# A four-layer graph network on one core: the written-out order of its operations set anew

## The chip, the cores and the metric

One core of one Trainium2 chip runs the whole program in one launch. The metric is device time in microseconds. Before the change the median of three runs is 2291.22 us (2289.76 to 2291.41).

The engines are named as in the profile: PE is TensorE's matmul, PEld its weight load, DVE is VectorE, ACT is ScalarE, POOL is GpSimd, and SP is SyncE, which here only issues DMAs.

## The reference

128 graphs of 64 nodes with 256 features (`x`), and an adjacency matrix per graph (`adj`), go through four layers. Each layer is followed by a residual and a layer norm. In float32, and cut to what matters:

```python
# layer 0: gated graph network, 5 steps
A = (adj != 0); h = x
for l in range(5):
    m = einsum('bnd,de->bne', h, weight[l])
    agg = einsum('bij,bid->bjd', A, m)
    h = gru_cell(agg, h, w_ih, w_hh, b_ih, b_hh)
x = layernorm(x + h * mask[..., None])
# layer 1: aggregate, two-layer network with an RMS norm between
agg = epsilon * x + adj @ x
h = silu(rmsnorm(agg @ W1 + b1, rms_weight))
x = layernorm(x + h @ W2 + b2)
# layer 2: tangent map, aggregate, map back onto the ball
x = layernorm(x + project(expmap0(adj @ logmap0(x))))
# layer 3: attention
h = x @ W_w.T + W_b
e, f = h @ a_w[:256], h @ a_w[256:]
u = adj * exp(e[:, :, None] + f[:, None, :] + a_b[0])
x = layernorm(x + (u / u.sum(2, keepdims=True)) @ h)
```

## The kernel before, in words

**Tiles and groups.** Two graphs share a block of 128 rows, so there are 64 blocks, and four blocks make a group: 16 groups. `group(g)` builds a group's operations. Layer 0 and most of layer 1 are built for all four blocks at once; the rest of the group is built twice, for a half of the blocks each. So the program is 49 streams: one for set-up and three per group. Buffers exist for three groups (`NF = 3`), and PSUM has eight banks of 512 columns that are handed out in turn.

**What a group does.** In layer 0, each of five steps (`gated`) aggregates (`ps_agg`, L396), multiplies by gate weights (`p_ga`, `p_gb`, `p_gc` at L915; `p_hx`, `p_hy`, `p_ix`, `p_iy` at L921), and evaluates sigmoids and tanh as tanh on ACT (L968, L1032). Products of 2 by 2 blocks are formed in seven products instead of eight, with sums on DVE (`tA`, `tB`, helper line L434) and additions of PSUM results on DVE (L965, L981, L937). The new state is made on DVE (L434, L1038, L1040), transposed in pieces on DVE (L877, `t`) and moved to rows by four DMAs (`hr`). Layer 1 uses `p_ah`, `p_bh`, `p_ch` (L1098), squares on ACT (L1084) that are summed on POOL (`sqt`, L437), Silu on ACT (L1149), and `p_ox`, `p_oy` (L1173). Layer 2 uses `ps_sup` and many small steps on POOL (`few`, L427; `few_s`, L431). Layer 3 uses `ps_a` and `ps_att`, with the small product at L1386. Layer norms take their sums from accumulators (L800, L817, L822), powers and small steps on POOL, and the scaling `x_n` on ACT or DVE (L419, L420). Additions of a bias row over a whole group run on POOL (`xb` and `x_n` at L437). The last two groups do the small steps on DVE instead, and the last group forms its second product of layer 1 without the seven-product scheme (`ps_o`).

**What sets the order.** No operation is emitted where the code names it. `flow.op` and `flow.either` only record it, in its stream, with an engine, a price in microseconds, what it reads and what it writes. `either` records an operation with two ways, ACT or DVE (`copied`, `scaled`, the `tan` scaling at L1293). When all is recorded, `flow.issue()` emits the operations in the order that the string `ORDER` (L58 to L243) spells, and binds each to the one before it on its engine by an ordering edge that needs no semaphore. Each engine then works through its own operations strictly in that order, and waits by semaphores for its inputs; SP issues its DMAs in that order too. The string is read so:

```python
for c in marks:
    i = at(next(marks)) * n + at(next(marks)) if c == "~" else at(c)
    i, e = divmod(i, len(self.ENGINES))
    i, s = divmod(i, self.AHEAD)
    o, eng = waiting[first + s][self.ENGINES[e]][i], self.ENGINES[e]
```

One mark thus names an engine `e`, a stream `s` counted from the first unfinished one, and the place `i` among the operations of that stream that may run on that engine and have not been taken. A mark of two letters after `~` has a larger number. An `either` operation goes to the engine that the mark names. The order in which PSUM banks are handed out follows the string as well. `placed()` uses neither the prices nor the `port` flags; they are what a planner outside the kernel was given to write the string with.

**The prices.** Before, `act` is priced at 0.22 + 0.00077 n whatever it reads, `scaled` at 0.3 + 0.0008 n on ACT, `dve` at 0.145 + 0.00105 n, `few` and `few_s` at 0.25, PE operations of 256 columns (two instructions each) at 0.433. A `port` flag marks a DVE or POOL operation[...].

## Time and profile before

| what | value |
|---|---|
| median of three runs | 2291.22 us |
| the profiled execution's own time | 2286.62 us |
| its span in the profile | 2284.8 us |
| mean granted PE clock | 0.996 of full speed |
| instructions | 34210 |
| operations in `ORDER` | 13729 |
| DMA traffic | 84.59 MB in 430044 packets |
| `hr` DMAs, issue to landing | 256 of 128 KB, median 3.8 us |
| ACT table loads | 47, 1.28 us each |

Times in the profile are microseconds unless marked ns. A row of a stretch gives its start and end, its length, then for PE, PEld, DVE, ACT and POOL the busy time with the number of instructions, the granted PE clock, the busy share of the DMA engines and the GB/s that they moved. A row in order of time gives start, length, engine, line, operation, output and inputs, and in brackets the idle time of the engine ahead of it with what ended it. A row of a group gives busy time and the mean ns of one, then the idle time ahead of the group. A line such as L437 or L419 belongs to a helper, so the tile names tell which operation is meant.

### The profile page before, as it was taken

The numbers are of one execution on the slowest core, as the hardware profiler recorded it, in microseconds if no ns is written. First come the engines' busy times: TensorE is split into PE (matmuls) and PEld (weight loads), VectorE is DVE, ScalarE is ACT, GpSimd is POOL, SyncE is SP. The second block draws the span as 40 slices with busy tenths as digits, with TensorE's granted clock in tenths as the row PEclk, the third lists the DMA queues.
The fourth block names the chain that finished last, engine by engine and source line by source line (L and its number), as shares of the span: only waits on it lengthen the run. The fifth ranks groups of instructions, "written<-read, shape, count | busy, mean of one in ns | idle before, by whom it ended". The sixth has DMA issues, their size and how long they took to land.

```text
span 2284.8 us, 34210 instructions
## 1 busy us (share of the span) xinstructions
PE 2237.4 (98%) x12050; PEld 1982.7 (87%) x12050; DVE 1827.1 (80%) x3832; ACT 1307.4 (57%) x2856; POOL 536.7 (23%) x827
## 2 busy tenths in 40 slices
PE   9999999999999999999999999999999999999986
PEld 7888898988898898988989889898988989888865
DVE  6787788787787888888888787878888788877886
ACT  3444656665556656556565666656566565654565
POOL 4100213422113213122231212222122231210222
PEclk9999999999999999999999999999999999999998
DMA  6021122112203122121212212212121212211110
GB/s 156 15 37 29 20 31 58 19 27 42 56 13 51 33 31 56 21 38 31 33 42 33 55 19 41 39 29 47 29 40 29 38 41 33 44 29 19 33 19 28
DMA packets 430044, 84.59 MB, mean 37 GB/s; under 512 B 399237, under 2 KB 428961, under 8 KB 429873
## 3 DMA queue, kind: packets, MB, share of 16 engines
q1 hardware_dynamic: 428144, 80.52, 19.9%
q8 instruction: 96, 1.57, 0.3%
q10 hardware_dynamic: 1328, 1.31, 0.2%
q0 software_dynamic: 400, 0.57, 0.1%
q14 instruction: 76, 0.61, 0.1%
HBM read 32.55 MB, written 8.39 MB: 18 GB/s over the span
## 4 chain that ended last, share of the span: by engine, by line
PE 89%; DVE 6%; DMA 1%; ACT 1%; SPq 1%; issue 1%; POOL 0%; ACTq 0%; DVEq 0%; POOLq 0%
PE p_ga L915 23%; PE p_gc L915 11%; PE ps_agg L396 7%; PE p_ix L921 6%; PE p_gb L915 6%; PE p_hx L921 6%; PE p_iy L921 5%; PE p_ox L1173 4%; PE p_hy L921 4%; PE p_ah L1098 4%; PE p_oy L1173 3%; PE ps_a L396 2%; PE p_ch L1098 2%; PE ps_sup L396 1%; PE ps_att L396 1%; PE p_bh L1098 1%
## 5 line engine op out<-in xcount | busy, mean ns | idle before, releaser
L431 POOL TENSOR_SCALAR mv<-st 128x4 f32<-128x4 f32 x56 | 17.5, 313 | 767.6 <-ACT x_n L817 425.2
L915 PE MATMUL p_ga<-hT,w_h 128*128 128x256 f32 x640 | 177.4, 380 | 0.9 <-DVE U L965 0.9
L915 PE MATMUL p_gc<-tA,w_h 128*128 128x256 f32 x640 | 177.4, 380 | 0.0
L915 PE MATMUL p_gc<-tB,w_a 128*128 128x256 f32 x640 | 176.1, 380 | 0.4 <-DVE tB L434 0.4
L915 PE MATMUL p_ga<-tA,w_h 128*128 128x256 f32 x640 | 175.7, 379 | 0.0
L915 PE MATMUL p_ga<-tB,w_a 128*128 128x256 f32 x640 | 171.1, 380 | 0.6 <-DVE tB L434 0.6
L915 PE MATMUL p_ga<-agg,w_a 128*128 128x256 f32 x640 | 170.4, 379 | 0.0
L396 PEld LDWEIGHTS ps_agg<-edge,hr 128*128 128x128 f32 x1024 | 146.2, 191 | 19.2 <-issue 4.9
L419 ACT ACTIVATE hnb<-p_hx,half_b 128x256 f32<-128x256 f32 x202 | 95.1, 472 | 105.7 <-PE p_hx L921 82.5
L968 ACT ACTIVATE U<-U,half_b 128x512 f32<-128x512 f32 (+1 forms) x160 | 94.4, 628 | 106.1 <-DVE U L965 105.9
L396 PE MATMUL ps_agg<-edge,hr 128*128 128x128 f32 x1024 | 150.6, 276 | 4.3 <-DMA hr<-t 2.8
L915 PEld LDWEIGHTS p_ga<-tB,w_a 128*128 128x128 f32 x640 | 120.1, 190 | 16.9 <-DVE tB L434 1.3
L915 PEld LDWEIGHTS p_gc<-tB,w_a 128*128 128x128 f32 x640 | 119.7, 190 | 16.9 <-DVE tB L434 1.2
L915 PEld LDWEIGHTS p_ga<-agg,w_a 128*128 128x128 f32 x640 | 119.1, 190 | 16.1 <-issue 0.7
L915 PEld LDWEIGHTS p_gc<-tA,w_h 128*128 128x128 f32 x640 | 119.0, 190 | 15.5 <-ACT agg L414 0.2
L915 PEld LDWEIGHTS p_ga<-hT,w_h 128*128 128x128 f32 x640 | 116.9, 190 | 15.2 <-DVE U L965 1.3
L915 PEld LDWEIGHTS p_ga<-tA,w_h 128*128 128x128 f32 x640 | 117.5, 190 | 14.2
L968 ACT ACTIVATE V<-V,half_b 128x256 f32<-128x256 f32 (+1 forms) x160 | 88.7, 587 | 68.0 <-DVE V L965 67.8
L834 POOL TENSOR_TENSOR rstd<-ve,pow 128x4 f32<-128x4 f32 (+2 forms) x67 | 80.2, 1197 | 136.2 <-DVE ve L832 124.8
L414 ACT COPY agg<-ps_agg 128x512 f32<-128x512 f32 x133 | 77.2, 582 | 51.1 <-PE ps_agg L396 50.0
L822 ACT ACTIVATE x_n<-y,mv 128x256 f32<-128x256 f32 x168 | 83.4, 499 | 38.4 <-POOL mv L431 38.4
L981 DVE TENSOR_TENSOR V<-p_ix,V 128x256 f32<-128x256 f32 x192 | 80.6, 420 | 27.9 <-PE p_ix L921 24.0
(289 smaller groups left out, 6161.1 us busy)
## 6 DMA issues: line engine op xcount, KB each, us to landing
hr<-t SPq DMA_DIRECT2D x256, 128.0 KB, 3.8
x<-in_x_dram SPq DMA_DIRECT2D x64, 128.0 KB, 2.6
xr<-in_x_dram SPq DMA_DIRECT2D x16, 512.0 KB, 3.5
xs<-in_x_dram SPq DMA_DIRECT2D x120, 64.0 KB, 2.4
out_dram<-x_n SPq DMA_DIRECT2D x15, 512.0 KB, 3.0
x3T<-t SPq DMA_DIRECT2D x56, 128.0 KB, 3.9
edge<-in_adj_dram SPq DMA_DIRECT2D x64, 32.0 KB, 2.5
wm<-in_L_gnn_weight_dram SPq DMA_DIRECT2D x5, 256.0 KB, 4.0
```

Source lines behind the costliest of these rows:

```text
L396: return nc.tensor.matmul(o, lhsT, rhs, start=(k == 0), stop=(k == nk - 1))
L414: flow.either([("ACT", 0.22 + 0.00077 * n, lambda: nc.scalar.copy(o(), i())), ("DVE", 0.145 + 0.00105 * n, lambda: nc.vector.tensor_copy(o ...
L419: flow.either([("ACT", 0.3 + 0.0008 * n, lambda: nc.scalar.activation(o(), i(), AF.Identity, bias=bias(), scale=scale())), ("DVE", 0.145 + ...
L431: pool(0.25, lambda: nc.gpsimd.tensor_scalar(w[0](), x(), s0, s1, op0, *((op1,) if op1 else ())), [w[1]], r)
L822: act(400, lambda b=b: nc.scalar.activation(o[:, b, :], y[:, at + b, :], AF.Square, bias=mv[:, b, 0:1], accum_out=st[:, b, 1:2]), [(o, b), ...
L834: pool(1.25, lambda: nc.gpsimd.tensor_tensor(rstd[:, :m, :], ve[:, :m, :], pow2[:, :m, :NB], OP.pow), [rstd], [ve])
L915: pe(HR, lambda i=i, w=w, c=c: nc.tensor.matmul(ps[:, c * HR:(c + 1) * HR], w[:, m, c * P:(c + 1) * P], v[i][0](), start=first and i == 1 ...
L921: pe(HR, lambda: nc.tensor.matmul(ps[:, j * HR:(j + 1) * HR], w[:, m, :], v[0](), start=first, stop=True, skip_group_check=True), [ps], [( ...
L968: act(HR if len(w) == 1 else R, lambda: nc.scalar.activation(o(), src(), AF.Tanh, bias=half_b[:, i * KD + c:i * KD + c + 1], scale=0.5), w ...
L981: dve(HR + 44, lambda: nc.vector.tensor_add(uu[:, c, half(n)], region(ps, j), uu[:, c, half(n)]), [(uu, (n, c))], [ps, (uu, (n, c))])
L1098: pe(HR, lambda c=c: nc.tensor.matmul(ps[:, c * HR:(c + 1) * HR], w1f[:, w, (2 * q + c) * P:(2 * q + c + 1) * P], v[0](), start=first and ...
L1173: pe(128, lambda j=j, k=k: nc.tensor.matmul(ps[:, i * HR + j * P:i * HR + (j + 1) * P], val(v[k // 2])[:, k % 2, j * P:(j + 1) * P], w2f[: ...
```

## The change

The string `ORDER` is replaced by another (18561 characters before, 18857 after). The set of operations and what each reads and writes stay as they are. Beside it, the prices are changed to durations measured in a trace, for ACT apart by whether an operand lies in PSUM (a bank) or in SBUF, and three operations get the `port` flag: the `edge` comparison (L862), the `tan` scaling on DVE and the small product at L1386. Prices and flags emit nothing.

The diff, with the first line alone of each string:

```diff
-    ORDER = ("EACAAEAg~BrADA#ECA~OX~BOAADAA$AADA$iAAC~N.~Bs~Bt~Bti~OXi~CU~CU~CU~CUi~Bt~Nr~B,~Bt8E8E~B,8l8~FU~Fy~Fy"
...
+    ORDER = ("CEEg~PhD~BNhED~BOiDC~Bs$CAAAAAAAAAAAAAAAAii~Nr~Nr~BO~N.~CU8~B+88~Bt~Bt8$~Bt~BL~Bt88li~BL~FU~FU~FU~FU"
...
+    def in_bank(r):
+        return any((a[0] if isinstance(a, tuple) else a).bank for a in r)
+
+    def on_act(n, r):
+        if n < 32:
+            return 0.26 if in_bank(r) else 0.205
+        return 0.355 + 0.00045 * n if in_bank(r) else 0.28 + 0.00085 * n
+
     def act(n, run, w, r, sets=None):
-        flow.op("ACT", 0.22 + 0.00077 * n, run, w, r, sets=sets)
+        flow.op("ACT", on_act(n, r), run, w, r, sets=sets)
...
     def scaled(n, o, i, scale, bias, w, r, port=()):
-        flow.either([("ACT", 0.3 + 0.0008 * n, ...),
-                     ("DVE", 0.145 + 0.00105 * n, ...)], w, r, port=port)
+        flow.either([("ACT", on_act(n, r) if in_bank(r) else on_act(n + 108, r), ...),
+                     ("DVE", (0.21 if in_bank(r) else 0.145) + 0.00105 * n, ...)], w, r, port=port)
...
     def few(w, x0, x1, op, r):
-        pool(0.25, ...)
+        pool(0.2, ...)
     def few_s(w, x, s0, op0, r, s1=None, op1=None):
-        pool(0.25, ...)
+        pool(0.23, ...)
...
     def pool_sum(n, o, x0, x1, op, w, r):
-        pool(0.24 + 0.00211 * n, ...)
+        pool(0.24 + 0.00203 * n, ...)
...
-            dve(R, lambda: nc.vector.tensor_scalar(ed[:, :NB, :], ...), [ed], [ed])
+            dve(270, lambda: nc.vector.tensor_scalar(ed[:, :NB, :], ...), [ed], [ed], True)
...
-                        dve(HR + 44, lambda: nc.vector.tensor_add(hnb[:, c, half(n)], ...
+                        dve(HR + 6, lambda: nc.vector.tensor_add(hnb[:, c, half(n)], ...
...
-                ("ACT", 0.43, ... tan ...),
-                ("DVE", 0.3, ... tan ...)], [(tan, b)], [(x2, b), fac])
+                ("ACT", 0.5, ... tan ...),
+                ("DVE", 0.35, ... tan ...)], [(tan, b)], [(x2, b), fac], port=("DVE",))
...
-            dve(4, lambda two=two: nc.vector.tensor_mul(rd[:, two], ...), parts, [...])
+            dve(4, lambda two=two: nc.vector.tensor_mul(rd[:, two], ...), parts, [...], True)
```

The remaining edits are of the same kind: powers on POOL from 1.25 to 0.41 + 0.625 for each of the one or two sets of values they take, and sizes in prices of transposes, squares and fused operations.

## The prediction

> **What bounds the kernel now.** I read the page's header and busy slices first, then the busy time by stretch, then the idle of PE by event, and last the rows of single operations.

> ```profile
> span 2284.8 us, 34210 instructions
> PE 2237.4 (98%) x12050; PEld 1982.7 (87%) x12050; DVE 1827.1 (80%) x3832; ACT 1307.4 (57%) x2856; POOL 536.7 (23%) x827
> PE   9999999999999999999999999999999999999986
> ```
> ```profile
> 0.00:60.00 60.00, 56.69 (x263) 43.17 (x264) 36.47 (x94) 18.83 (x46) 27.95 (x44) 1.00 0.59 148
> 60.00:120.00 60.00, 59.52 (x289) 50.84 (x288) 43.59 (x90) 24.64 (x50) 6.22 (x8) 1.00 0.12 19
> 120.00:2200.00 2080.00, 2059.55 (x11163) 1837.97 (x11162) 1685.04 (x3417) 1210.93 (x2636) 485.35 (x756) 1.00 0.20 35
> 2200.00:2284.00 84.00, 61.63 (x340) 50.72 (x339) 62.01 (x233) 53.01 (x125) 17.21 (x19) 0.90 0.06 20
> ```
> PE is the bound. The stretches give its idle time: 3.3 us in the first 60, 0.5 in the next 60, 20.5 between 120 and 2200, 22.4 after that, and 0.8 in the last piece: 47.4 in all. Busy PE is not PE at its peak, so I also worked out a floor from the chain of waits, where 16 matmuls on 256 columns take 3.45 us (0.2156 each) and 16 on 128 columns take 1.78 (0.111).
> ```profile
> 98.24 3.45 PE p_ga L915 x16
> 356.53 1.78 PE ps_agg L396 x16
> ```
> The rows by shape hold 8168 matmuls 256 to 258 wide (1761 us), 3714 of 128 or less but over one (413), 40 of 512 at twice 0.2156 (17), and 128 of one column at 0.10 (13): 2204 us. The span is 81 us above it, 47 visible and 34 hidden. A hidden part follows each stall: a matmul's modelled end (0.38 us) trails the next one's earliest start by 0.16 us. So a new order can gain at most some 80 us (3.5%), and of this the lonely end of the last group holds about half.

> Between 60 and 2180 the visible idle is 23 stalls of 0.17 to 1.60 us, 16.2 us together. Three kinds stand out. First, a VectorE operation stretched beside a long GpSimd sum:
> ```profile
> 1170.77 2.35 POOL L437 TENSOR_TENSOR xb<-x_n,b_r 128x1024 f32<-128x1024 f32 x1 [0.22 <-DMA x<-in_x_dram]
> 1170.93 2.48 DVE L862 TENSOR_SCALAR edge<-edge 128x512 f32<-128x512 f32 x1 [2.00 <-PE ps_adjT L857]
> 1174.06 1.13 PE L1098 MATMUL p_bh<-aggm,w1f 128*128 128x256 f32 x4 [0.99 <-DVE aggm L415]
> ```
> The `edge` operation took 2.48 us; in another place (1447.17) the same one took 0.42. The same picture ends in stalls at 1020.8 (0.87), 1032.9 (0.95), 1063.6 (0.92), 1449.9 (0.40), 1853.9 (1.09), 1879.5 (0.63), 1980.6 (0.36): eight stalls, 6.2 us. Second, waits for the DMAs that bring `hr` and `x3T`, 5 stalls, 3.6 us. Third, plain lateness of DVE or ACT, the other ten, 6.4 us.

> [...]

> **The change part by part.** The program of instructions is built from `ORDER` alone; the prices and the port flags in the diff emit nothing. I cost them at zero, and read them for what the new order was made to believe.
> ```profile
> L1149 ACT ACTIVATE hid<-hid,cols 128x512 f32<-128x512 f32 x128 | 84.7, 715 | 2.8 <-DVE hid L1147 2.6
> L419 ACT ACTIVATE hnb<-p_hx,half_b 128x256 f32<-128x256 f32 x202 | 95.1, 472 | 105.7 <-PE p_hx L921 82.5 <-DMA hr<-t 21.5 <-PE p_ga L915 0.4
> L414 ACT COPY agg<-ps_agg 128x512 f32<-128x512 f32 x133 | 77.2, 582 | 51.1 <-PE ps_agg L396 50.0
> L1386 DVE TENSOR_TENSOR few<-few,hw 128x2 f32<-128x2 f32 x32 | 10.6, 333 | 1.0
> L431 POOL TENSOR_SCALAR few<-few 128x4 f32<-128x4 f32 x126 | 34.5, 275 | 9.9
> L427 POOL TENSOR_TENSOR few<-few 128x4 f32<-128x4 f32 x126 | 32.1, 255 | 14.3 <-ACT few L1317 4.9
> ```
> *ACT prices.* From SBUF at 512 the old price is 0.22 + 0.00077 x 512 = 0.614, the new 0.28 + 0.00085 x 512 = 0.715, the row 0.715; seven such groups have 576 instructions, so the old plan missed 576 x 0.101 = 58 us of ACT. From PSUM at 256 with a bias the old is 0.505, the new 0.470, the row 0.472; a copy of 512 from PSUM was 0.614, is 0.585, row 0.582. The old plan thus put ACT too early behind SBUF work and too late behind PSUM. DVE additions of 256 from PSUM (some 800) go from 0.460 to 0.420, rows 0.417 to 0.421. These are now right to within 0.01 us.

> *Port flags.* `edge` (L862), `tan` (L1295) and the small product at L1386 are marked[...]. L1386's mean of 333 ns hides single ones of 1.2 to 1.9. Four of the eight port stalls are of just these two: 1032.9, 1174.1, 1449.9 and 1853.9, 3.4 us. I take all four as gone, because the new order was made with that conflict known. It could be from none (engines run free of each other, so an order cannot forbid an overlap) to all.

> *The order itself.* Decoded by `placed()`'s rule, both strings hold 13729 operations: PE 6210 in both, POOL 821, SP 615; DVE goes from 3615 to 3629, ACT from 2468 to 2454. So 14 copies or scalings move from ACT to DVE, at 0.4 to 0.69 us each: at most 10 us on a DVE that has 458 us free, beside PE's work; on the path at zero, but up to 3 us if they fall where DVE is already the late one. After each 275 operations the count of PE operations in the two strings agrees within 3. So no stage is moved: it is local shuffling, also of SP's DMA issues, where a moved issue passes others on SP's queue and a waiting one holds up those behind it.

> *Middle, 60 to 2200.* Idle 20.9. The four flagged stalls go, 3.4. Of the remaining 17.5 I take half, 8.7: lateness from wrong ACT and DVE prices can be planned away, that from DMA landings (no price of theirs is in the diff) less so. From both sides: nothing, or all of it. Some 15 stalls less also free 15 x 0.16 = 2.4. Against this I set 2 us of new stalls: each one in the list is 0.7 on average, so three new ones. Sum: -12.5.

> *Start.* 2.55 of its 3.3 idle us is PE waiting for the identity matrix, which no order changes. -0.5.

> *End.* 22.4 us idle with the clock at 0.90, a chain of one group's last layers: ACT, DVE and small POOL steps in series, and 80 matmuls of `ps_o` with nothing to put beside them. Filling it asks that other groups' work be left for it. -4, between +2 and -12.

> Sum: -17. Against the profiled execution's own 2286.62 (span 2284.8 and 1.8 around it) that is 2269.6; its time lies 4.6 under the median of the runs, 2291.22, and I take the same difference there: **2274**.

> **The rivals.** About 0.2% (4.6 us) is what a measurement here can tell from no change.
> (a) *The likeliest*, stalls thinned as above: 2264 to 2284, its middle 2274. For it: prices now agree with the rows. Chance 0.50.
> (b) *More than that*: nearly all the middle goes (-20 with the hidden part) and the end is half filled (-11), with 3 more from hidden pieces: -34, 2257. Against it: the end's chain is serial. 0.13.
> (c) *Stalls only change places*, or the shuffling does not act on what limits: the 3.4 us and what else goes comes back as new waits, 2290. For it: the old order too was made to have no stalls and has 23; DMA landings are as uncertain as before. 0.13.
> (d) *Slower, through GpSimd's small steps.* The new prices are 0.20 and 0.23 where the rows measure 0.255 and 0.275; the old 0.25 fitted. There are 504 of them, in the chains of the layer norms and of the tangent map, so the plan lets every chain end early: 504 x 0.05 = 25 us of lateness over the run. POOL itself is 23% busy; but `x_n`, `tan` and the additions behind them sit in DVE's and ACT's queues, in order, and block what follows there, PE's evacuations included. If some 0.6 of it reaches PE (+15) and only the four flagged stalls are gained (-3.4): 2303. It decides over the gain when over two thirds (17 of 25) come through. [...] 0.24.

> **How the numbers follow.** Faster 0.50 + 0.13 = 0.63; same 0.13; slower 0.24. The range runs from (b) to (d), 2256 to 2303: I leave 0.06 below and 0.12 above.

> **What would show it.** Right: visible idle of PE between 60 and 2200 near 10 us; no L862 or L1386 over 1 us; ACT and DVE counts as decoded. The end: idle after 2200 near 18. Wrong: idle in the middle at 20 or above, with releasers `x_n`, `tan` or `y` behind POOL rows (d), or DMA `hr` (c); or a longer end that takes back the middle's gain.

## The result, and the profile after

| | median us | range | runs | against before |
|---|---|---|---|---|
| before, beside the changed kernel | 2289.14 | 2287.16 to 2291.47 | 20 | |
| changed kernel | 2286.86 | 2281.24 to 2288.74 | 20 | 0.9988 [0.9981, 0.9995] |

The change gains 2.3 us, 0.12%: inside the band of 0.2% that the prediction called no change, where 17 us had been forecast. (The three runs of before that the prediction starts from are among these 20; their median, 2291.22, lies 2 us above that of all.) The profiled execution of the changed kernel took 2287.12, its span is 2284.7; that of before took 2286.62, so these two executions differ by next to nothing, and the comparisons below show where time moved, not what the change is worth. Its header, busy times and PE slices:

```profile
span 2284.7 us, 34183 instructions
PE 2239.7 (98%) x12050; PEld 1983.1 (87%) x12050; DVE 1827.2 (80%) x3846; ACT 1304.0 (57%) x2842; POOL 533.6 (23%) x827
PE   8999999999999999999999999999999999999987
```

VectorE has 14 instructions more and ScalarE 14 fewer, as decoded. The first slice of PE went from 9 to 8. The same four stretches as before say where:

```profile
0.00:60.00 60.00, 52.95 (x242) 39.36 (x243) 36.02 (x87) 17.44 (x44) 25.06 (x41) 0.97 0.54 148
60.00:120.00 60.00, 60.00 (x293) 51.41 (x292) 41.99 (x88) 26.16 (x53) 7.63 (x11) 1.00 0.09 14
120.00:2200.00 2080.00, 2064.09 (x11176) 1840.76 (x11175) 1686.56 (x3440) 1206.32 (x2618) 483.76 (x756) 1.00 0.20 35
2200.00:2284.00 84.00, 62.67 (x345) 51.56 (x343) 62.61 (x236) 54.08 (x127) 17.16 (x19) 0.89 0.06 19
```

PE's idle time is 7.1 us in the first 60 (3.3 before), 15.9 between 60 and 2200 (20.9), 21.3 after that (22.4). So three stages moved by +3.8, -5.0 and -1.0. In the first stage the clock is 0.97 as well, where before had 1.00. I also took each stretch's length less the matmuls that start in it at the prediction's steady prices (0.2156 us for 256 to 258 columns, 0.431 for 512, 0.111 for 128, 0.10 for one), so that hidden losses count:

| us above that floor | 0 to 60 | 60 to 2160 | 2160 to the end |
|---|---|---|---|
| before | 7.5 | 34.4 | 39.6 |
| after | 12.0 | 29.9 | 39.5 |

The middle gained 4.5 and the start gave it back. Single executions differ, but not by that much: in the first 60 us the old start is 7.5 to 10.5 us above the floor in all seven profiles of kernels that have it, the new one 12.0 to 13.3 in three.

**The middle.** PE's waits between 60 and 2200 by what ended them, longest sums first (total us, times, longest), after:

```profile
PE ps_hr L782 <- DVE hT L1051: 3.5, 3, 1.9
PE ps_agg L399 <- DMA hr<-t: 3.2, 5, 0.9
PE ps_a L399 <- DMA x3T<-t: 1.6, 2, 0.9
...
PE p_hx L932 <- ACT hnb L430: 0.8, 1, 0.8
```
and before:
```profile
PE ps_hr L771 <- DVE hT L1040: 3.5, 2, 2.6
PE ps_agg L396 <- DMA hr<-t: 2.8, 3, 1.2
PE ps_att L396 <- DVE y L800: 2.0, 2, 1.1
PE p_hx L921 <- ACT hnb L419: 1.6, 1, 1.6
```

Of the waits for late VectorE and ScalarE work, those of `ps_att` for `y` are gone, that for `hnb` is halved and the one at the top, for `hT`, is as long as before; those for DMAs grew from 3.6 to 4.8. And VectorE is still held by GpSimd. The place of the prediction's example, after, in order of time:

```profile
1171.76 2.37 POOL L448 TENSOR_TENSOR xb<-x_n,b_r 128x1024 f32<-128x1024 f32 x1
1172.38 0.69 DVE L426 COPY adjT<-ps_adjT 128x512 f32<-128x512 f32 x1 [0.28 <-PE ps_adjT L868]
1172.99 1.42 DVE L873 TENSOR_SCALAR edge<-edge 128x512 f32<-128x512 f32 x1
...
1175.76 1.10 PE L1109 MATMUL p_ch<-ts,w1f 128*128 128x256 f32 x4 [0.38 <-DVE ts L445]
...
1838.19 2.36 POOL L448 TENSOR_TENSOR x_n<-x_n,wb_r 128x1024 f32<-128x1024 f32 x1 [5.33 <-DVE t L1366]
1838.36 2.47 DVE L445 TENSOR_TENSOR tB<-tB,agg 128x256 f32<-128x256 f32 x1
1842.21 0.44 PE L782 MATMUL ps_hr<-ident,hT 128*128 128x128 f32 x2 [0.88 <-DVE hT L1051]
```

The new order put a copy that reads PSUM (0.69, not held) ahead of `edge`, so that `edge` is held for less: 1.42 instead of 2.48. But it still ends at 1174.41, 0.28 after GpSimd's sum. `tB`, an addition that has the `port` flag in both kernels, is held to 1840.83, again 0.28 after the sum beside it, where the same shape elsewhere takes 0.42. Between 60 and 2200 single VectorE operations of 1.5 us or more went from 17 to 12, no further. All twelve lie beside a GpSimd sum and end 0.02, 0.28 or 0.55 us after it, by whether they take 0.16, 0.42 or 0.69 us alone: always 0.14 less than their own time. So the rows look like a wait followed by a run of the usual length, not like a slower pace.

Which operations wait can be told from the traces. Of those that start inside a GpSimd sum of 512 or 1024 columns with 0.9 us or more of it to go, in the profiles of before and of the changed kernel, 52 of the 53 with two inputs in SBUF were held, and all four `edge` comparisons, which have one; none of the 147 that read PSUM was, nor any of 11 transposes and 5 reciprocals, which read and write SBUF alone. The one that was not held, a `V` at 1718.73 in the changed kernel, started 0.01 us after the sum and took 0.68; that sum took 2.91, where 23 of the 30 of its shape take 2.34 to 2.38.

**The start.** PE's only wait of over 0.15 us between 10 and 60 us in the profile before:

```profile
23.26 0.70 PE L921 MATMUL p_hx<-tA,w_hn 128*128 128x256 f32 x2 [0.31 <-DVE tA L434]
```

VectorE, PE and GpSimd from 24 us on, in the profile after:

```profile
24.31 1.93 DVE L536 TENSOR_TENSOR w_in<-w_in 128x128 f32<-128x128 f32 x3
26.15 0.41 DVE L445 TENSOR_TENSOR tA<-hT,tA 128x256 f32<-128x256 f32 x1
26.60 1.37 DVE L445 TENSOR_TENSOR tA<-tA,hT 128x256 f32<-128x256 f32 x1
```
```profile
26.62 1.11 PE L932 MATMUL p_hx<-tA,w_hn 128*128 128x256 f32 x2 [2.25 <-DVE tA L445]
...
32.98 0.70 PE L932 MATMUL p_hx<-hT,w_hn 128*128 128x256 f32 x2 [1.16 <-DVE hnb L948]
```
```profile
24.82 1.26 POOL L681 TENSOR_TENSOR w2f<-w2f 128x512 f32<-128x512 f32 x1 [16.42 <-DMA w2f<-in_L_gnn_W_dram]
26.27 4.24 POOL L681 TENSOR_TENSOR w2f<-w2f 128x512 f32<-128x512 f32 x3 [0.18 <-DMA w2f<-in_L_gnn_W_dram]
```

GpSimd's sums of `w2f`, released by DMAs, lie on VectorE's small sums; PE waits 2.25 us for `tA` and then runs at half clock, as single microseconds show (the clock is the third figure from the end):

```profile
26.00:27.00 1.00, 0.38 (x1) 0.38 (x2) 0.96 (x3) 0.00 (x0) 0.81 (x2) 0.88 1.08 378
27.00:28.00 1.00, 1.00 (x4) 0.74 (x4) 1.00 (x2) 0.23 (x1) 1.00 (x2) 0.50 0.88 239
```

### The profile page after: what moved, and what is told of

Read it like the earlier page. It is cut to its first block, busy times and chain, and to the rows that moved or that the text cites. A ratio compares the mean times of both kernels' runs of the same rounds, so it can differ in the third digit from the quotient of the medians.

```text
span 2284.7 us, 34183 instructions
## 1 busy us (share of the span) xinstructions
PE 2239.7 (98%) x12050; PEld 1983.1 (87%) x12050; DVE 1827.2 (80%) x3846; ACT 1304.0 (57%) x2842; POOL 533.6 (23%) x827
## 4 chain that ended last, share of the span: by engine, by line
PE 92%; DVE 4%; DMA 2%; SPq 1%; ACT 1%; issue 1%; POOL 0%; POOLq 0%; DVEq 0%; ACTq 0%
PE p_ga L926 23%; PE p_gc L926 11%; PE ps_agg L399 7%; PE p_ix L932 6%; PE p_hx L932 6%; PE p_gb L926 6%; PE p_ah L1109 5%; PE p_iy L932 4%; PE p_ox L1184 4%; PE p_hy L932 4%; PE p_oy L1184 3%; PE p_ch L1109 2%; PE ps_a L399 2%; PE ps_wmih L399 1%; PE ps_sup L399 1%; DMA hr<-t 1%
## 5 line engine op out<-in xcount | busy, mean ns | idle before, releaser
L979 ACT ACTIVATE U<-U,half_b 128x512 f32<-128x512 f32 (+1 forms) x160 | 95.1, 629 | 91.2 <-DVE U L976 91.2
L1184 PE MATMUL p_oy<-w2f,hid 128*128 128x128 f32 x720 | 101.1, 278 | 0.5 <-ACT hid L1160 0.4
```

What stands on the lines that cost most here:

```text
L979: act(HR if len(w) == 1 else R, lambda: nc.scalar.activation(o(), src(), AF.Tanh, bias=half_b[:, i * KD + c:i * KD + c + 1], scale=0.5), w ...
L1184: pe(128, lambda j=j, k=k: nc.tensor.matmul(ps[:, i * HR + j * P:i * HR + (j + 1) * P], val(v[k // 2])[:, k % 2, j * P:(j + 1) * P], w2f[: ...
```

## The experiments

Each kernel was timed in five rounds beside before, whose medians in the four sets were 2289.05, 2289.39, 2289.71 and 2289.73. In brackets is the 95% interval of the ratio; 0.001 is 2.3 us.

| kernel | median us | runs | ratio to before |
|---|---|---|---|
| start_new | 2294.15 | 10 | 1.0021 [1.0012, 1.0030] |
| middle_new | 2282.70 | 9 | 0.9974 [0.9965, 0.9984] |
| end_new | 2287.88 | 13 | 0.9993 [0.9985, 1.0001] |
| split_sums | 2276.17 | 5 | 0.9948 [0.9935, 0.9962] |
| before_split | 2277.49 | 5 | 0.9949 [0.9937, 0.9962] |
| split_cols | 2279.11 | 5 | 0.9956 [0.9944, 0.9969] |
| start_sp_old | 2288.83 | 13 | 0.9998 [0.9990, 1.0007] |
| start_dve | 2293.15 | 14 | 1.0017 [1.0009, 1.0025] |
| start_pool_late | 2290.98 | 21 | 1.0007 [1.0001, 1.0014] |
| start_wm_first | 2287.77 | 13 | 0.9992 [0.9984, 1.0000] |
| after_wm_first | 2282.22 | 6 | 0.9965 [0.9953, 0.9978] |
| best1 | 2272.51 | 5 | 0.9930 [0.9916, 0.9943] |
| best2 | 2271.55 | 5 | 0.9922 [0.9910, 0.9935] |
| best3 | 2271.27 | 5 | 0.9919 [0.9905, 0.9933] |

**Which stage, alone.** The two orders hold the same set of operations after 589 and after 12533 of the 13729, so they can be joined there.

```diff
 start_new:  operations 1-589 new | 590-13729 old
 middle_new: 1-589 old | 590-12533 new | 12534-13729 old
 end_new:    1-12533 old | 12534-13729 new
```

> The new order for the first 589 operations alone (to about 100 us), the old order after that. Theory A (the start gives back what the middle gains: VectorE's sums for tA wait for a DMA and run beside GpSimd's w2f sums, PE idles over 2 us and its clock drops): visible idle of PE in the first 60 us near 7 us against 3 of the old order, clock below 1.00 there, and 3 to 6 us slower than before, ratio 1.0013 to 1.0026. Theory B (the start differs by chance from execution to execution, and the stalls of the middle only changed places): within 1.5 us of before.

> The new order for operations 590 to 12533 alone (about 100 to 2100 us), the old order for the start and the end. Theory A: 5 to 8 us faster than before, ratio 0.9965 to 0.9978; visible idle of PE between 60 and 2160 near 12 us against 17. Theory B: faster by 1 to 3 us, as the whole change is.

> The new order for the last 1196 operations alone (from about 2100 us), the old order before that. Theory A and theory B: the end's chain is serial and no order of these operations changes it, so within 1.5 us of before. If the end is over 2 us slower or faster, both are wrong on it and the sum of the three parts has to be redone.

Measured +5.1, -6.35 and -1.2 us; together -2.4, the whole change's -2.3. The parts add up, so each can be explained by itself; that they do so to 0.1 us is luck, with intervals of some 2 us either way. The end's -1.2 is not told from nothing.

**Is VectorE held by GpSimd's instruction?** In `pool_sum`, with the new order (split_sums) and with the old one (before_split):

```diff
-        pool(0.24 + 0.00203 * n, lambda: nc.gpsimd.tensor_tensor(o(), x0(), x1(), op), w, r)
+        def run():
+            if n < 1024:
+                return nc.gpsimd.tensor_tensor(o(), x0(), x1(), op)
+            return [nc.gpsimd.tensor_tensor(o()[:, b, :], x0()[:, b, :], x1()[:, b, :], op) for b in range(4)]
+        pool(0.24 + 0.00203 * n, run, w, r)
```

> The new order whole, with each of the 30 GpSimd sums of 128 x 1024 issued as four of 128 x 256, in the same place. Theory A (what is left of the middle's idle time comes from VectorE operations held for as long as one GpSimd sum runs, which no order prevents): no VectorE operation of the middle is held over 1.5 us beside these sums, PE's visible idle between 60 and 2160 falls from 12 to 7 to 9 us, and the time falls by 3 to 5 us against the new order. Theory B (the hold is of the whole stretch, or the idle time is that of serial chains): no VectorE row changes much, within 1.5 us of the new order, or slower by the four times 0.2 us of extra instructions on GpSimd's chains.

> The old order, with each of the 30 GpSimd sums of 128x1024 issued as four of 128x256. Theory: a VectorE operation is held until the GpSimd instruction beside it ends, so shorter ones release it earlier whatever the order is; the old order has eight such stalls, 6.2 us of visible idle, and hidden parts beside them, so it gains as much as the new one did (10.7) or a little less: 2278 to 2281. Rival: the split gains because the new order was set with these overlaps in mind; then the old one gains under 5 us, 2284 or more.

split_sums is 10.7 us under the changed kernel, over twice what was expected; before_split 11.9 us under before. So the gain does not depend on the order. Four sums of 256 take longer than one of 1024 (30 sums: 72.5 us before, 90.1 split, as the groups of 128x1024 and 128x256 add up), but a VectorE operation is let go after the piece beside it. The same `edge` beside such pieces in before_split:

```profile
1166.71 1.59 POOL L440 TENSOR_TENSOR xb<-x_n,b_r 128x256 f32<-128x256 f32 x2 [0.22 <-DMA x<-in_x_dram]
1166.80 0.93 DVE L866 TENSOR_SCALAR edge<-edge 128x512 f32<-128x512 f32 x1 [2.00 <-PE ps_adjT L861]
```

It took 0.93 where it took 2.48. Operations of 1.5 us or more: 17 in before, 9 of them beside the sums of 1024; in before_split the 9 are gone and 7 are left, all beside the 512-wide sums of `sqt`, which were not cut. The loss above the floor between 60 and 2160 fell from 34.4 to 25.2. Another reading was open: a reader of one block may start when that block's piece is done. Cutting by columns excludes it, since every block then needs all four pieces:

```diff
-            return [nc.gpsimd.tensor_tensor(o()[:, b, :], x0()[:, b, :], x1()[:, b, :], op) for b in range(4)]
+            return [nc.gpsimd.tensor_tensor(*(v()[:, :, 64 * q:64 * q + 64] for v in (o, x0, x1)), op) for q in range(4)]
```

> The old order, with each GpSimd sum of 128x1024 issued as four of 128x256, but cut by columns (64 of the 256 columns of all four blocks) instead of by blocks. Theory (a VectorE operation is held to the end of the GpSimd instruction beside it): the cut does not matter, 2276 to 2280, like the cut by blocks (2277.49). Rival: the cut by blocks gains because readers of a finished block can start before the whole sum is done; here every block is complete only with the fourth piece, so this stays at 2286 to 2290.

It gains 10.6 us. Early release is not the cause; whether it adds the 1.3 us by which the cut by blocks gained more, the intervals can't tell.

**What in the start costs 5.1 us?** My first theory was VectorE's own sequence. Two kernels, each start_new with one engine's queue put back, all of SP's, or 17 of VectorE's operations (the sums for `tA` and `tB` ahead of the second transpose and of another group's `tA`):

```diff
 start_sp_old, SP:  62 DMAs in the old sequence
 start_dve, DVE:
-hT, hT, tA, tB, tB, tA (next group), w_in x3, tA, tA, tB, ...
+hT, tB, tA, tB, w_in, tB, tA, w_in, tA, w_in, hT, tA (next group), ...
```

> The new order for the first 589 operations with the old order after them, but SP issues its DMAs of this part in the old order. The new start alone cost 5.1 us (2294.15 against 2289.05). Theory: what costs is VectorE's new sequence, which puts a second transpose, another group's first sum and three weight sums ahead of the tA that PE waits for (2.31 us at 25.7); the DMAs only add to it, so this kernel stays at 2292 to 2294. Rival: the early w2f transfers cost, since they start GpSimd's w2f sums at 26.2 beside those VectorE operations (in the old start at 29.8 to 31.3) and delay x and xs; then it comes back to 2289.5 to 2290.5, and the PE wait on tA falls under 1 us.

> The new order for the first 589 operations with the old order after them, but with 17 VectorE operations in the neighbourhood of 20 to 31 us in the old sequence: first one transpose, the four sums of tA and tB that PE waits for, then the second transpose, the other group's first sum and most of the weight sums. Theory (VectorE's own sequence): the PE wait of 2.31 us on tA falls under 0.7, the clock stays at 1.00 through the first 40 us, and the time is 2290 to 2291.5, 3 to 4 us under the new start's 2294.15. Rival (early DMAs and the GpSimd sums that they start): the tA sums are held all the same; wait 1.5 or more, 2293 to 2295.

The theory fell. SP's old sequence takes the cost away (2288.83); VectorE's leaves 3.8 us of it. In start_dve `tA` was in time, and PE waited for what came next, a `wm` DMA and then `hnb` behind held weight sums:

```profile
29.03 0.63 PE L628 MATMUL ps_wmT<-ident,wm 128*128 128x128 f32 x4 [1.77 <-DMA wm<-in_L_gnn_weight_dram]
32.39 1.22 PE L922 MATMUL p_hx<-hT,w_hn 128*128 128x256 f32 x2 [2.30 <-DVE hnb L938]
```

The new order has two `w2f` DMAs ahead of two `wm` ones that they follow in the old. The next two kernels take apart what that does: late `wm`, or early GpSimd sums.

```diff
 start_wm_first, SP:
 w2f
-w2f
 edge
-w2f
 wm
 wm
+w2f
+w2f
 start_pool_late, POOL:
-w2f x4
 w_a and w_in x7
+w2f x4
```

> The new order for the first 589 operations with the old order after them, and on SP's queue one move: the two w2f DMAs that the new order put ahead of two of the wm weight DMAs go behind them. With SP's whole queue in the old order the start's cost was gone (2288.83), with VectorE's alone hardly (2293.15: PE then waited 1.77 us for a wm DMA and 2.30 for hnb behind VectorE sums that lay beside GpSimd's w2f sums). Theory A (late wm): the wm wait goes and the GpSimd sums start later too: 2289 to 2290.5. Theory B (order elsewhere on the queue, x and w1f moved too): 2292 or more, with the wm wait replaced by one for x or w1f.

> The new order for the first 589 operations with the old order after them, and on GpSimd's queue one move: the four w2f sums go behind its first seven sums of w_a and w_in, so that none runs before 39 us; the DMAs are as in the new order. Theory B (the sums beside VectorE do the harm): no VectorE operation between 24 and 32 us over 1 us, the PE wait for tA (2.31 us) under 1, the clock at 1.00 there, 2289 to 2291. Theory A (late wm landing, and x): the waits for tA shorten by the holds, but PE then waits for wm: 2292 to 2294.

One move of two DMAs takes back all of it: 2287.77, 6.4 us under start_new. Moving only the sums takes back 3.2 us (2290.98), or 3.8 of the 5.1 when each kernel is set against the before beside it: the wait for `tA` is then 0.90 us and no VectorE sum is held. That part is shown. For the rest I had late `wm` data in mind, which stay late in this kernel, but its profile has only 0.41 us of PE waiting for them, and it shows another loss. From 42 to 53 us PE is, matmul for matmul, 4.5 us ahead of where it is in start_new and only 0.4 behind start_wm_first. Then it waits 2.72 us, which it does in neither of the other two, and its clock is at 0.50 for 3.4 us:

```profile
55.10 0.42 DVE L718 TENSOR_TENSOR a_t<-a_t 128x256 f32<-128x256 f32 x1 [5.10 <-DMA a_t<-in_L_gnn_a_w_dram]
56.25 2.24 PE L397 MATMUL ps_wmih<-wihT,wmT 128*128 128x256 f32 x6 [2.72 <-DVE w_a L421]
```

VectorE's `w_a` stood behind a sum of `a_t`, whose DMA GpSimd itself issues (at 51.47; at 51.05 in start_new, where PE was that much later). So in these profiles the early sums are nearly the whole cost, late `wm` data at most 0.4 us, and the move made a loss of its own. The profile is that of the slowest of 21 executions, 4.7 us above their median, so how much of this loss the others have stays open. SP's rows for the two tensors, in the changed kernel and in start_wm_first:

```profile
20.76 1.15 SPq L684 DMA_DIRECT2D w2f<-in_L_gnn_W_dram  x2
22.62 0.59 SPq L684 DMA_DIRECT2D w2f<-in_L_gnn_W_dram  x1
23.26 1.02 SPq L572 DMA_DIRECT2D wm<-in_L_gnn_weight_dram  x2
```
```profile
21.31 0.59 SPq L674 DMA_DIRECT2D w2f<-in_L_gnn_W_dram  x1
22.61 1.10 SPq L562 DMA_DIRECT2D wm<-in_L_gnn_weight_dram  x2
23.76 1.02 SPq L674 DMA_DIRECT2D w2f<-in_L_gnn_W_dram  x2
```

In start_wm_first GpSimd's four sums run from 28.88, after the VectorE sums that they held; PE's wait for `tA` is 1.24 us and its clock stays at 1.00. The same move in the whole change:

> The whole change with one move: on SP's queue the two w2f DMAs that stand ahead of two wm DMAs go behind them. In the new start alone that move took 2294.15 to 2287.77. Theory (the start of the whole change loses by the same two DMAs): 2286.9 less 5 to 6.5, 2280 to 2282, and the clock at 1.00 up to 40 us. Rival (the start's cost depends on what follows it, or the gain of the middle was partly the other side of it): 2284 or more.

Its gain over before is 7.5 us where the change alone had 2.3, so the move is worth about 5.2 there too, at the low end of what was expected.

**Joined.** best1 is the split sums with the old start and the new order after it. best2 adds to it transposes that keep PE busy while the last group waits; best3 is best2 with the repaired new start.

```diff
+            def held(p, b, n, real):
+                return [nc.tensor.transpose(p[:, i % 4 * P:(i % 4 + 1) * P], ident.tile(), ident.tile())
+                        for i in range(n if b == 0 and g == NG - 1 else 0)] + [real()]
```

> The split GpSimd sums in the new order, with the first 589 operations in the old order. If the start's cost (5.1) and the split's gain (10.7) add, this is 2276.2 - 5.1 = 2271, 2269.5 to 2272.5. Rival: the lost clock in the first 60 us came by chance of the run and the start is worth under 2: 2274 to 2276.

> The old start, the new order after it, split sums (2272.51 so far), and in the last group 12, 12 and 20 more transposes of the identity matrix ahead of the first ps_ss, ps_rms and ps_o matmul, written into the bank that the real one then overwrites; they need no input and run while PE waits there (1.41, 1.37 and 2.25 us). Theory: the ps_o matmuls run at 0.54 of the full clock in 2220 to 2224 because PE was idle before; kept busy, they save 1.5 to 2.5 us, 2270 to 2271. Rival: ps_o is fed by ACT (hid) anyway, so a faster PE only waits: 2272 to 2273.

> The whole change with the two w2f DMAs behind the wm ones, the GpSimd sums split by blocks, and the transposes that keep PE busy in the last group's waits: best2 (2271.55) with the repaired new start for the old one. The repaired start was 2287.77 where the old one has 2289.4, so 2269.5 to 2271.5. Rival: no difference between the two starts, 2271.5 to 2272.5.

best1 gains 3.7 us more than split_sums, at the upper edge of what was expected. best2 and best3 are 1.0 and 1.2 us under it, with intervals that overlap, so neither the added transposes nor the repaired start (0.3 us between the two) is told from nothing here. The profile shows why the transposes bring so little: the clock between 2214 and 2224 went from 0.66 in best1 to 1.00 in best3:

```profile
2214.00:2224.00 10.00, 5.90 (x31) 5.45 (x31) 6.00 (x12) 7.72 (x19) 3.42 (x5) 0.66 0.00 0
```
```profile
2214.00:2224.00 10.00, 9.11 (x74) 8.07 (x73) 5.91 (x12) 8.26 (x19) 3.42 (x5) 1.00 0.00 0
```

yet in best3 a quick `ps_o` then waits for ScalarE's `hid`:

```profile
2219.62 1.82 PE L399 MATMUL ps_o<-w2f,hid 128*128 128x128 f32 x12
2222.25 13.31 PE L399 MATMUL ps_o<-w2f,hid 128*128 128x128 f32 x116 [0.81 <-ACT hid L1169]
```

best3, 2271.27 us, is 18.5 us (0.8%) under before and 15.6 under the changed kernel.

## Why the prediction was wrong

- **PE is the bound, some 80 us above a floor of 2204:** right. The gaps above the floor add up to 81.5 us before and 81.4 after, in the two executions profiled.
- **Decoded counts, no stage moved:** right, and the two orders even meet exactly at many places.
- **The sum, -17 against -2.3:** the start is 5.6 us worse than predicted, the middle 6.2 and the end 2.8.
- **Start, -0.5:** this step failed, and it turned the result: the new start costs 5.1 us. The prediction saw that SP's DMA issues were moved and that "a moved issue passes others on SP's queue", but priced none of them. Two `w2f` issues passed two `wm` issues. Most of the harm, 3.2 to 3.8 us by the times and 4.5 by PE's rows, came from what they set going early on GpSimd: sums that hold VectorE, an idle PE, and half its clock for 3.4 us.
- **Middle, -12.5:** right in sign, too large: -6.35 alone. The four flagged stalls, 3.4 us, did not all go; 0.9 are left, with `edge` up to 1.51 us and the small product up to 2.05. That a flag ends an overlap was assumed, and the old order spoke against it: the operations behind the other four of the eight stalls beside GpSimd sums (`hT`, `V`, `tB`), which the prediction calls port stalls, have the flag in both kernels, and in before the `tB` at 1977.94 took 2.58 us beside such a sum. Of the remaining waits up to 2180 the plain lateness fell from 6.4 to 2.9, about the half that I took. But the half was applied to all 17.5, and the other classes did not fall: stalls behind held operations that had the flag already 2.8 before and 3.1 after (0.8 of these is a wait at 1559.60 for a `V` behind a held `tA`, which the prediction, at 0.4, had put under lateness), DMA waits 3.6 and 4.8. The 2.4 us of hidden gain did not show: the gap above the floor fell by 4.5, the visible idle between 60 and 2160 by 4.7.
- **Port stalls priced at 6.2 us:** too low. Splitting GpSimd's sums in the old order is worth 11.9. There the gap above the floor fell by 9.2 between 60 and 2160, the visible idle by 7.0: more than the eight stalls that I counted beside GpSimd sums, and hidden pieces with them. 2.5 us more went in the end.
- **End, -4:** -1.2 alone, not told from nothing by its interval; idle 21.3 us instead of 18.
- **The rivals.** (d) did not happen: GpSimd's small steps measure 269 and 266 ns, and no wait of PE ends on one in the middle. (c) has the time, but not its mechanism: stalls did go in the middle, only that the start took them back; its part on DMA landings holds (+1.2). For this band I had given 0.13.

## What to carry to other kernels

When an order is made anew, compare each queue pair by pair at the start, where PE waited 1.77 us for a late `wm` in start_dve, and ask of every DMA issued earlier which engine it sets going, and beside which other engine's operations that one then runs: the early `w2f` sums cost 3.2 to 3.8 us here. In the two profiles of before and after, VectorE operations with two inputs in SBUF, and the `edge` comparison with one, were held to the end of the GpSimd sum beside them (56 of 57), while those that read PSUM, transposes and reciprocals were not (none of 163); the new order shortened such holds in places and left them in others, while cutting the 128x1024 GpSimd sums into four took 10.6 to 11.9 us out under either order. Join old and new order at points where both have done the same operations: the parts' times added up here, well within their intervals.

## What the hardware showed unexpectedly

- After 2.25 us without a matmul, with little idle before it, PE ran at 0.50 of its clock from 26.8 to 30.2 us. But a gap of 1.40 us in after_wm_first left the clock at 1.00, and so did one of 2.58 in before:

```profile
2193.65 0.66 PE L771 MATMUL ps_hr<-ident,hT 128*128 128x128 f32 x4 [2.58 <-DVE hT L1040]
```
